# Row sums of a self-attention layer: partial sums kept by DMAs are added on VectorE instead of being summed by TensorE, and the DMAs' blocks lie two to three places earlier

## The chip, the cores and the metric

The kernel runs on one core of one Trainium2 chip. The metric is device time in microseconds, the median of several runs of the same program. Three runs of the kernel before took 3301.09, 3304.72 and 3309.56 us.

## The reference

Two layers work on an image batch `x` of shape (2, 256, 64, 64). Each is `x = x + layer(groupnorm(x))`. Layer 1 (block attention and a 3x3 convolution) is not touched here. Layer 0 is full self-attention over the 4096 pixels of each image, with 8 heads of 32 channels:

```python
qkv = jnp.einsum('bchw,oc->bohw', x, qkv_w) + qkv_b[None, :, None, None]
qkv = qkv.reshape(b, 3, num_heads, head_dim, n)
q, k, v = (qkv[:, 0], qkv[:, 1], qkv[:, 2])
attn_logits = jnp.einsum('bhci,bhcj->bhij', q, k) * scale
attn_weights = jax.nn.softmax(attn_logits, axis=-1)
out = jnp.einsum('bhij,bhcj->bhci', attn_weights, v)
```

The softmax needs, for each query, the sum of its 4096 exponentials. How these sums are taken is the subject.

## The kernel before

**Units, blocks, groups.** For one image, layer 0 is cut into 16 groups `g`: head `g // 2` and one half of the queries (2048 of them, in 4 units `u` of T = 512). A group has NJ = 32 blocks `j`, each of 128 keys. Block `j` of a group is four *units*: score tiles of 128 keys x 512 queries. For each unit TensorE makes the scores (L426) into PSUM, ScalarE takes the exponential of two or three units at once (L432), and TensorE multiplies the result with the values (L442, tile `av`). That last product has only 32 output rows, so the four units of a block are written to four quarters of one PSUM bank (`quarters`, L438). The two images follow one another, so layer 0 has 32 groups in all; layer 1 of each image comes after its layer 0.

**The ring.** Exponentials lie in a ring of 28 places (RING, L378), which is seven blocks or four batches of scores. A place is written again four batches later, so by then everyone who reads it must be done: TensorE, VectorE, and DMAs.

**The row sums.** Summing over the 4096 keys has two steps. First, the 32 blocks of a group are added element by element, so that 128 x 512 partial sums stay for each unit. Then a product with a matrix of ones sums over the 128 partitions. The element-by-element part is split in two:

- VectorE adds most blocks into two tiles `added[g]` (`e` in the profile, L471 to L479), two units (128 x 1024) in one instruction.
- The seven blocks in `SUMMED` (L380) are added by DMAs that accumulate, issued from GpSimd (`add_in_memory`, L481): the first of a group is a plain copy (L487), the others add (L489). They go to four buffers `acc`, which lie in tiles of several names, so the profile calls them `es`, `v` and `acc`.

`sum_rows` (L502) then multiplies both with `ones`: one product of four quarters for `acc`, one for `added`, into one spare bank of the score tile `sa`. In the last group of an image `finish_last` (L538) does the same with two blocks more.

**What follows.** `finish(g)` (L509) takes the row sums on: ScalarE copies them out (L515), a DMA brings them to DRAM and back in a dense form (L516, L518), VectorE takes minimum, maximum and reciprocal (L521 to L523), DMAs bring the reciprocals back, spread over partitions (L524, L526), and VectorE multiplies the group's output with them (L530). Each of these steps has its place in the next group: the sums after block 1 has been worked on, the reciprocal after block 8, the multiplication after block 13.

**The order of work.** `tc.manual_schedule` (L635) keeps the order in which instructions are written for TensorE, ScalarE and VectorE. The loop at L643 writes one batch of 7 units of scores and exponentials, then as many steps of older blocks as a fixed share allows (`steps`, L609). [...] SyncE's queue has the plain DMAs: in even groups it fetches the next head's keys and values at block 4 (L622, `fetch_head`), and at the end of each group the queries of the group after the next (L631).

Around the change, the sums of group `g` are asked for after block 1 of group `g + 1` (L615), and are written once two more steps have been written, which is at block 3 or 4. `waiting` is a check of the program's writer: `acc` may not be overwritten before the sums have read it.

Of the kernel before, what the change touches and what calls it, by code (L numbers as in the profile page):

```python
# [40 lines left out]
def direct_layers(ctx: ExitStack, tc: tile.TileContext, a: dict, out: bass.AP, bad: bass.AP):  # L41
# [3 lines left out]
    nc = tc.nc  # L45
# [13 lines left out]
    def w4(shape, name, dtype=F32):  # L59
        return work.tile(shape, dtype, tag="w4", name=name)  # L60
# [159 lines left out]
    ones = const.tile([P, HD0], F32, name="ones")  # L220
# [81 lines left out]
    def fetch_head(b, h, held):  # L302
        r = slice(HD0 * h, HD0 * h + HD0)
        kt = kpool.tile([P, N], F32R, tag="kv", name=f"k_{b}_{h}")
        for g in range(4):
            nc.sync.dma_start(
                out=kt[HD0 * g : HD0 * g + HD0, :].bitcast(F32), in_=halves["wk0"][b][g // 2, r, :]
            )
        held["k", h] = kt
        nc.sync.dma_start(out=held["v"][:, h % 2, :, :], in_=vals[b][:, :, r])  # L310

    def fetch_queries(b, g, held):
        h, p = divmod(g, 2)
        r = slice(HD0 * h, HD0 * h + HD0)
        for w in range(2):
            qt = w4([P, 2, T], f"q_{b}_{g}_{w}", F32R)
            n0 = (4 * p + 2 * w) * T
            for q in range(4):
                nc.sync.dma_start(
                    out=qt[HD0 * q : HD0 * q + HD0].rearrange("p s n -> p (s n)").bitcast(F32),  # L320
                    in_=halves["wq0"][b][q % 2, r, n0 : n0 + 2 * T],
                )
            held["q", g, w] = qt
# [53 lines left out]

    RING, RING_A = 28, 17  # L378

    SUMMED = (5, 9, 13, 17, 21, 25, 28)  # L380


    SUMMED_LAST = (NJ - 2, NJ - 1)

    def attention0(b, xts, held):
# [6 lines left out]
        pair = cpool.tile([P, 2, T], F32, tag="col", name=f"acc_{b}")  # L392

        acc = [es[:, RING_A, :], held["acc"][:, 0, :], pair[:, 0, :], pair[:, 1, :]]
        vals2 = held["v"]
        n_units = NH0 * 2 * NJ * 4
        sums, added, copied = {}, {}, {}
        waiting = []
        last = NH0 * 2 - 1
# [4 lines left out]
        def at_places(first, n):  # L404

            while n > 0:
                at = first % RING
                m = min(n, (RING_A if at < RING_A else RING) - at)
                yield m, es[:, at : at + m, :] if at < RING_A else held["es"][:, at - RING_A : at - RING_A + m, :]
                first, n = first + m, n - m  # L410
# [27 lines left out]
        def quarters(dst, lhs, rhs, start, stop, part=None):  # L438

            n = slice(0, T) if part is None else slice(part * T // 2, (part + 1) * T // 2)  # L440
            for u in range(4):
                nc.tensor.matmul(dst[HD0 * u : HD0 * u + HD0, n], lhs, rhs(u)[:, n], start=start, stop=stop)  # L442

        def unit(g, j, u):
            ((_, e),) = at_places(places[(g * NJ + j) * 4 + u], 1)
            return e[:, 0, :]
# [10 lines left out]
        def add_rows(g, j):  # L457
# [4 lines left out]
            for w in range(2):  # L462
                dst = added[g][w]
                if j in SUMMED:
                    if w == 0:
# [15 lines left out]
        def add_in_memory(g, j):  # L481
            assert not waiting or j != SUMMED[0]
            runs = [(acc[u].unsqueeze(1), unit(g, j, u).unsqueeze(1)) for u in (0, 1)]
            runs += [(pair[:, s, :], src) for s, src in two_units(g, j, 1)]
            for dst, src in runs:
                if j == SUMMED[0]:
                    nc.gpsimd.dma_start(out=dst, in_=src)  # L487
                else:
                    nc.gpsimd.dma_start(out=dst, in_=src, accum_op=ALU.add)  # L489

        def work_of(g, j):


            add_rows(g, j)
            for part in (None,) if j in (0, NJ - 1) else range(2):
                if part == 1:
                    yield
                quarters(
                    sums[g], held["v"][:, (g // 2) % 2, j, :], lambda u: unit(g, j, u), j == 0, j == NJ - 1, part
                )  # L500

        def sum_rows(g, rows):  # L502
            waiting.clear()
            quarters(rows, ones, lambda u: acc[u], True, False)
            for j in SUMMED_LAST if g == last else ():
                quarters(rows, ones, lambda u: unit(g, j, u), False, False)
            quarters(rows, ones, lambda u: added[g][u // 2][:, u % 2, :], False, True)

        def finish(g):  # L509

            h, p = divmod(g, 2)
            rows = yield
            sum_rows(g, rows)
            avs = copied[g]
            nc.scalar.copy(avs[:, 1, :], rows)  # L515
            nc.sync.dma_start(out=dsum[b][g], in_=avs[0:P:HD0, 1, :])  # L516
            dense = small.tile([P, 4 * T // P], F32, tag="dense", name=f"dense_{b}_{g}")
            nc.sync.dma_start(out=dense, in_=dsum[b][g].rearrange("u (q n) -> (u q) n", n=4 * T // P))  # L518
            yield
            at = b * NH0 * 2 + g  # L520
            nc.vector.tensor_reduce(span[:, 0, at : at + 1], dense, AX.X, ALU.min)  # L521
            nc.vector.tensor_reduce(span[:, 1, at : at + 1], dense, AX.X, ALU.max)
            nc.vector.reciprocal(dense, dense)  # L523
            nc.sync.dma_start(out=drec[b][g].rearrange("u (q n) -> (u q) n", n=4 * T // P), in_=dense)  # L524
            for u in range(4):
                nc.sync.dma_start(  # L526
                    out=avs[HD0 * u : HD0 * u + HD0, 1, :], in_=drec[b][g, u].partition_broadcast(HD0)
                )
            yield
            nc.vector.tensor_mul(avs[:, 0, :], avs[:, 0, :], avs[:, 1, :])  # L530
            for u in range(4):
                nc.sync.dma_start(
                    out=ctx0[b][HD0 * h : HD0 * h + HD0, (4 * p + u) * T : (4 * p + u + 1) * T],
                    in_=avs[HD0 * u : HD0 * u + HD0, 0, :],
                )
            yield
# [72 lines left out]
        def steps():  # L609

            for done in range(NH0 * 2 * NJ):
                g, j = divmod(done, NJ)
                for _ in work_of(g, j):
                    yield done
                if g and j == 1:  # L615
                    wanted.append(late[0].send)
                    waiting.append(g)
                if g and j in (8, 13):
                    next(late[0])
                for what in also.get((g, j), ()):  # L620
                    what()
                if j == 4 and g % 2 == 0 and g // 2 + 1 < NH0:  # L622
                    fetch_head(b, g // 2 + 1, held)
                if j == NJ - 1:
                    avs = w4([P, 2, T], f"avs_{b}_{g}")
                    nc.scalar.copy(avs[:, 0, :], sums[g])
                    copied[g] = avs
                    late[:] = [finish(g)]
                    next(late[0])
                    if g + 2 < NH0 * 2:  # L630
                        fetch_queries(b, g + 2, held)  # L631
                yield done + 1

        E = mybir.EngineType
        with tc.manual_schedule(engines={E.PE, E.Activation, E.DVE}):  # L635

            per_group = 2 * NJ - 2
            work, begun, taken = steps(), 0, 0  # L640
            scores(False)
            final = False
# [977 lines left out]
def kernel(tc: tile.TileContext, a: dict, out: bass.AP):  # L1620
    nc = tc.nc
    with tc.tile_pool(name="verdict", bufs=1) as verdict:
        bad = verdict.tile([1, 1], I32, name="bad")
        direct_layers(tc, a, out, bad)
        redo = nc.values_load(bad[0:1, 0:1])
        with tc.If(redo > 0):
            general_layers(tc, a, out)
# [79 lines left out]
```

## Time and profile before

The profiled execution has a span of 3295.2 us. Layer 0 of the two images runs from about 110 to 1175 us and from about 1757 to 2817 us. Both stretches look alike.

| Stretch (us) | Length | PE busy | DVE busy | ACT busy | POOL busy |
|---|---|---|---|---|---|
| 190 to 1140, layer 0, first image | 950 | 941.18 | 817.89 | 876.32 | 256.54 |
| 1160 to 1760, layer 1 and projections | 600 | 537.55 | 347.21 | 200.46 | 135.24 |
| 1760 to 2809, layer 0, second image | 1049 | 1042.47 | 906.49 | 969.18 | 285.57 |
| 2809 to 3295, layer 1, second image | 486 | 433.44 | 210.00 | 143.28 | 119.09 |

A row of such a table is read across: the engine whose busy time comes closest to the length is the first suspect for the bound of that stretch, and the others show how much room they have. In the lists of groups, a line names the code line, engine, operation, tiles and shapes, then how many there were, their busy time in us and the mean of one in ns, and, after the second bar, the idle time just before them with what ended it.

### The profile page before, as it was taken

To read this page: it belongs to the slowest core of one execution; us is meant where nothing else is said; L and a number is where in the kernel's file an instruction comes from. 1 tells how busy PE (TensorE), PEld (TensorE's weight loads), DVE (VectorE), ACT (ScalarE), POOL (GpSimd) and SP (SyncE) were. 2 spreads that over 40 slices of the span, in tenths; PEclk is the share of its full clock that TensorE was granted. 3 is DMA by queue.
4 is the path that set the end of the run, shared out by engine and by line. 5 is a ranking of instruction groups with operands and counts; after the bars stand their busy time and mean duration, and the time that the engine had idled before them with its cause. 6 is when DMAs were issued, how large, how long until landed. Compare 5 with 4: busy or idle time off the path is not lost. (4 is left out here: it accounts for less than half of the span.)

```text
span 3295.2 us, 62532 instructions
## 1 busy us (share of the span) xinstructions
PE 3139.2 (95%) x25113; PEld 1844.7 (56%) x25113; DVE 2416.1 (73%) x3138; ACT 2310.7 (70%) x2354; POOL 843.4 (26%) x929
## 2 busy tenths in 40 slices
PE   7999999999999979999979999999999999799998
PEld 4455555555555535666654555555555555356665
DVE  4688888888989888554446887978889898424454
ACT  2798999999989943422227999999999999424222
POOL 2122222223222210444201222222222222005331
PEclk9999999999999979999989999999999999799999
DMA  7967878689776631300159678787797776200000
GB/s 258 251 136 152 168 144 181 145 158 183 143 163 139 141 76 47 134 26 26 45 187 255 137 153 171 142 175 153 158 185 144 156 145 139 79 2 10 14 13 27
DMA packets 243917, 425.23 MB, mean 129 GB/s; under 512 B 99009, under 2 KB 109593, under 8 KB 241185
## 3 DMA queue, kind: packets, MB, share of 16 engines
q0 software_dynamic: 98336, 241.20, 37.8%
q1 hardware_dynamic: 145280, 179.93, 20.5%
q8 instruction: 199, 3.26, 0.4%
q14 instruction: 102, 0.83, 0.1%
HBM read 118.26 MB, written 67.86 MB: 56 GB/s over the span
## 5 line engine op out<-in xcount | busy, mean ns | idle before, releaser
L479 DVE TENSOR_TENSOR e<-e,es 128x1024 f32<-128x1024 f32 (+1 forms) x950 | 1034.4, 1149 | 57.2 <-ACT es L432 57.0
L442 PE MATMUL av<-es,v 128*32 128x256 f32 (+1 forms) x9644 | 745.6, 390 | 0.0
L432 ACT ACTIVATE es<-sa 128x1536 f32<-128x1536 f32 (+1 forms) x444 | 635.6, 1431 | 92.3 <-PE sa L426 47.7
L479 DVE TENSOR_TENSOR e<-e,v 128x1024 f32<-128x1024 f32 (+1 forms) x630 | 668.9, 1118 | 22.7 <-ACT v L432 22.3
L426 PE MATMUL sa<-q,k 128*128 128x512 f32 x1736 | 561.1, 430 | 13.7 <-issue 4.5
L442 PE MATMUL av<-v 128*32 128x256 f32 (+1 forms) x6228 | 506.9, 389 | 0.0
L442 PEld LDWEIGHTS av<-es,v 128*32 128x32 f32 x9644 | 316.2, 109 | 299.4 <-issue 160.2
L426 PEld LDWEIGHTS sa<-q,k 128*128 128x128 f32 x1736 | 279.9, 188 | 297.0 <-issue 139.9
L426 PE MATMUL sc<-q,k 128*128 128x512 f32 x1180 | 373.1, 397 | 7.2 <-ACT es L432 4.3
L426 PE MATMUL sb<-q,k 128*128 128x512 f32 x1180 | 371.3, 396 | 2.1 <-ACT es L432 1.6
L442 PEld LDWEIGHTS av<-v 128*32 128x32 f32 x6228 | 216.3, 109 | 178.5 <-issue 81.5
L432 ACT ACTIVATE es<-sc 128x1024 f32<-128x1024 f32 x296 | 306.8, 1037 | 3.8 <-DVE e L479 3.8
L432 ACT ACTIVATE v<-sc 128x1024 f32<-128x1024 f32 x294 | 304.9, 1037 | 0.4 <-DMA es<-v 0.2
L432 ACT ACTIVATE es<-sb 128x1024 f32<-128x1024 f32 x296 | 302.1, 1021 | 2.9 <-DMA acc<-es 2.9
L432 ACT ACTIVATE v<-sb 128x1024 f32<-128x1024 f32 x294 | 300.1, 1021 | 2.6 <-DMA acc<-v 1.4
L426 PEld LDWEIGHTS sc<-q,k 128*128 128x128 f32 x1180 | 209.0, 187 | 83.6 <-ACT es L432 17.3
L426 PEld LDWEIGHTS sb<-q,k 128*128 128x128 f32 x1180 | 220.2, 188 | 59.0 <-ACT es L432 4.1
L489 POOL DMA_DIRECT2D es<-es x118 | 101.4, 859 | 523.4 <-ACT es L432 468.5
L801 POOL TENSOR_TENSOR v<-col 128x512 f32<-128x512 f32 x128 | 167.0, 1330 | 264.7 <-DMA out_dram<-res_sr 116.9
L432 ACT ACTIVATE v<-sa 128x1536 f32<-128x1536 f32 (+1 forms) x146 | 209.2, 1433 | 33.4 <-PE sa L426 15.2
L811 PE MATMUL mm<-v,wf 128*128 128x256 f32 x1024 | 226.6, 379 | 2.2 <-POOL v L801 1.2
L816 ACT COPY z<-mm 128x512 f32<-128x512 f32 x32 | 18.7, 585 | 283.8 <-PE mm L811 268.3
(241 smaller groups left out, 3519.0 us busy)
## 6 DMA issues: line engine op xcount, KB each, us to landing
acc<-es POOLq DMA_DIRECT2D x122, 512.0 KB, 6.1
acc<-v POOLq DMA_DIRECT2D x76, 512.0 KB, 6.3
es<-es POOLq DMA_DIRECT2D x136, 256.0 KB, 3.8
v<-es POOLq DMA_DIRECT2D x132, 256.0 KB, 4.6
k<-wk_halves SPq DMA_DIRECT2D x64, 512.0 KB
q<-wq_halves SPq DMA_DIRECT2D x256, 128.0 KB
v<-v POOLq DMA_DIRECT2D x92, 256.0 KB, 4.8
es<-v POOLq DMA_DIRECT2D x88, 256.0 KB, 3.8
```

The lines of the kernel that those rows point to most:

```text
L426: nc.tensor.matmul(sc[:, i, :], held["k", g // 2][:, j * P : (j + 1) * P], held["q", g, u // 2][:, u % 2, :], start=True, stop=True,)
L432: nc.scalar.activation(dst, sc[:, i : i + m, :], AF.Exp, scale=SC0)
L442: nc.tensor.matmul(dst[HD0 * u : HD0 * u + HD0, n], lhs, rhs(u)[:, n], start=start, stop=stop)
L479: nc.vector.tensor_add(dst[:, s, :], dst[:, s, :], src)
L489: nc.gpsimd.dma_start(out=dst, in_=src, accum_op=ALU.add)
L801: (nc.gpsimd.tensor_add if plus else nc.gpsimd.tensor_sub)(dst, rows(one), rows(two))
L811: nc.tensor.matmul(mm[:, m, r, :], wf[:, k, 4 * r + q, m * P : (m + 1) * P], v[r // 2][:, r % 2, k, :], start=k == 0, stop=k == KC - 1,)
L816: nc.scalar.copy(z[:, 1], mm[:, :, 1, :])
```

## The change

The list `SUMMED` moves forward: 5, 9, 13, 17, 21, 25, 28 becomes 3, 7, 11, 15, 18, 22, 26. There are still seven blocks in it. In every group but the last of an image, `sum_rows` no longer multiplies `acc` with ones; instead VectorE, at block 0 of the next group, adds `acc` into `added` with three instructions (two of 128 x 512 and one of 128 x 1024), and the one remaining product reads `added` alone. The last group of an image keeps its two products (and those of its last two blocks). The `waiting` check follows the new reader of `acc`.

```diff
-    SUMMED = (5, 9, 13, 17, 21, 25, 28)
+    SUMMED = (3, 7, 11, 15, 18, 22, 26)
...
         def sum_rows(g, rows):
-            waiting.clear()
-            quarters(rows, ones, lambda u: acc[u], True, False)
-            for j in SUMMED_LAST if g == last else ():
-                quarters(rows, ones, lambda u: unit(g, j, u), False, False)
-            quarters(rows, ones, lambda u: added[g][u // 2][:, u % 2, :], False, True)
+            if g == last:
+                quarters(rows, ones, lambda u: acc[u], True, False)
+                for j in SUMMED_LAST:
+                    quarters(rows, ones, lambda u: unit(g, j, u), False, False)
+            quarters(rows, ones, lambda u: added[g][u // 2][:, u % 2, :], g < last, True)
...
                 for _ in work_of(g, j):
                     yield done
+                if g and j == 0:
+
+                    for w in range(2):
+                        dst = added[g - 1][w]
+                        for s in range(2) if w == 0 else (slice(0, 2),):
+                            nc.vector.tensor_add(dst[:, s, :], dst[:, s, :], acc[s] if w == 0 else pair)
+                    waiting.clear()
                 if g and j == 1:
                     wanted.append(late[0].send)
-                    waiting.append(g)
...
                 if j == NJ - 1:
+                    waiting.append(g)
                     avs = w4([P, 2, T], f"avs_{b}_{g}")
```

## The prediction

> **What bounds the kernel now.** I read three views in this order: busy time by stretch, for the engine that has no room; the groups of instructions by line, for the price of one; the timeline of a group's seam and of a wait, for what hides what.
>
> ```profile
> 190.00:1140.00 950.00, 941.18 (x9172) 528.40 (x9174) 817.89 (x835) 876.32 (x835) 256.54 (x313) 1.00 0.78 155
> 1760.00:2809.00 1049.00, 1042.47 (x10149) 587.49 (x10149) 906.49 (x912) 969.18 (x916) 285.57 (x349) 1.00 0.79 158
> ```
>
> Columns: stretch, length, then busy us (and instructions) of PE, PE's weight loads, DVE, ACT, POOL, then clock, DMA share, GB/s. In the first layer-0 stretch PE is busy 941.18/950 = 99%, ACT 92%, DVE 86%. Starts of L515 in the timeline (row sums copied out, once per group) lie (2755.86 - 1836.52)/14 = 65.7 us apart, that is 2.05 us per block. Per group ACT works 0.922 x 65.7 = 60.6 us, DVE 0.861 x 65.7 = 56.6 us. So **PE bounds layer 0**; ACT has 5 us of room per group and DVE 9.
>
> ```profile
> 586.55 0.59 PE L442 MATMUL sa<-v,ones 128*32 128x512 f32 x1
> 587.40 1.04 PE L442 MATMUL sa<-e,ones 128*32 128x512 f32 x8
> 588.26 0.61 PE L442 MATMUL av<-v 128*32 128x256 f32 x8
> ...
> 588.51 0.58 ACT L515 COPY avs<-sa 128x512 f32<-128x512 f32 x1 [0.82 <-PE sa L442]
> ...
> 590.04 6.89 DVE L479 TENSOR_TENSOR e<-e,es 128x1024 f32<-128x1024 f32 x6
> ```
>
> This is the seam of one group (start, duration, what). The product of `acc` starts at 586.54, that of `e` at 587.40, the next `av` at 588.26: each ones-product holds PE for 0.86 us, back to back, with no wait in it. The last line gives the DVE's pace: six adds in 6.89 us, so (6.89 - 1.215)/5 = 1.135 us each when they follow one another, 2.27 us per block of two, **more than the 2.05 us in which a block is made**. DVE falls behind in a run of its own blocks and catches up at those that DMAs add.
>
> ```profile
> DVE avs L530 <- DMA avs<-drec: 145.7, 24, 10.6
> ...
> POOL es L487 <- PE sa L442: 519.5, 30, 19.9
> ...
> 810.73 0.69 DVE L530 TENSOR_TENSOR avs<-avs 128x512 f32<-128x512 f32 x1 [9.98 <-DMA avs<-drec]
> ...
>   DVE e L479: 10.9, 16
> ```
>
> First two: waits by pair (total us, times, longest). At block 13 the DVE stands still for the reciprocals, 6.1 us on average in 24 of 30 groups, with adds queued behind. The third is one such wait, 9.98 us in an even group, where the fetch of the next head (issued at block 4) is ahead of `drec`. The last is from the list of what ended ACT's idle time at L432: 16 waits for a DVE add, 10.9 us in all, since a place of the ring was still being read. They lie just after such waits (L530 ends at 811.4; blocks 14 to 20 of that group are done within 0.1 to 1.3 us of their place's next writing). So DVE is already at its limit in some even groups, but only there.
>
> [...] I checked the steps: 0.2166 us each, and over the 258 batches of scores of each image the time above the median batch comes to only 13.1 and 6.5 us. The trace agrees that PE really is issuing. [...] the four quarters start within 0.02 us, and a product's 8 instructions cost two steps of 0.43, not eight. [...]
>
> **The change, part by part** (against the profiled span, 3295.2 us).
>
> 1. *Product of `acc` removed.* Groups of L442: 240 `sa<-e,ones` over 8 per product = 30 groups; the same 240 for `acc` (120 + 60 + 60) go. 30 x 0.86 = **-25.8 us**, on the path. The rest of the seam follows: ACT's copy L515 waited 0.82 us for PE, 24.4 us in 30, so it can start 0.8 us sooner; at most 0.05 us a group is lost to ACT.
>
> 2. *Three adds on DVE per group.* 0.68 + 0.68 + 1.14 = 2.50 us (rows of L479), 30 groups, 75 us. DVE then needs 59.1 of 64.8 us per group. Hidden? They stand between block 31 and the next group's first add. PE needs `added` at its ones-product: from the DVE's end of block 31 to the first ones-product I read 3.4 us (first image, group 2) to 12.3 us, so 0.9 us stays at the worst: **0**. Behind them, blocks 0 and 1 come 2.5 us later; the tightest place there has 2.97 us until its next writing (group 11). From block 3 on, which DVE no longer adds, it is level again: before the reciprocal at block 8 it now does six blocks and the three adds, in place of seven blocks (+0.2 us).
>
> 3. *New wait: DVE's adds on the landing of the last accumulation,* with the whole DVE queue behind. POOL's last issue of block 28 ended 5.3 to 12.0 us before DVE finished block 31; block 26 is two blocks, 4.1 us, sooner. So 9.4 us or more, against a landing of 6.0 (longest 12.4): **0**; at worst 3 us in a few groups where DVE has no backlog.
>
> 4. *DMA blocks moved.* Nothing is removed: seven blocks, three or four POOL issues each. The first of a group (L487) waited for PE's product (519.5 us in 30, harmless); now it waits for DVE's adds. Block 3's exponentials and the adds are both done 9.7 to 14 us before the ring needs the places; the seam, shorter by 0.86, lies inside that. Issue takes 1.7 us and landing 6.0, so some 1.1 us stays in the tightest (groups after even ones); a landing of 12.4 would stall up to 5. I take **+1 us** in all, bounds 0 and 12. Past SP's queue: the accumulations near the head fetch were those of blocks 5, 9 and 13, now 3, 7 and 11; about two still fall into it.
>
> 5. *DVE blocks around the wait at block 13.* Before it come 9, 10, 12, 13 in place of 10, 11, 12: one block, 2.27 us, more work inside a wait of 6.1, which pays most of the 75 us (24 x 2.27 = 54). After it block 14 is as late as before, but every following block has one add fewer ahead of it. The ring waits of 10.9 us shrink: **-2 us**, bounds 0 and -11.
>
> Sum: -25.8 + 0 + 0 + 1 - 2 = -26.8, so 3268.4 for the profiled span. That execution lies 9.5 us under the median of 3304.7 (its spread is 8.5); from the median: **3278 us**.
>
> **Rivals.**
>
> - *More:* ring waits vanish too, -37: **3267**. For: later blocks gain 2.27 us. Against: block 14 gains nothing.
> - *Half:* block 3's accumulations land late, or the worst seams have DVE behind; about 1 us in each of 12 groups: **3290**. For: the 0.9 and 1.1 us left over. Against: these are single groups; most keep 3 us.
> - *No gain:* ACT or DVE is right behind PE, so what PE saves is waited away: **3304**. For: ACT at 92%. Against: 5 us of room, and ACT's waits at L432 are mostly for PE.
> - *Slower:* the reciprocals come later in even groups[...]. There are 12 such groups, and there DVE is at the ring's limit, so each us goes to PE. Break-even at 25.8/12 = 2.2 us; a delay of 4 us costs 48 - 26 = +22: **3327**. For: waits of 7 to 10 us there show a crowded queue. Against: blocks 5 and 9 met the same fetch, as many bytes.
> - *That the change does nothing* would need the `acc` product to lie in idle PE time; the seam shows none.
>
> **How the numbers follow.** Forecast (3271 to 3285) 62%, more 14%, half 13%, no gain 5%, slower 6%. Range 3266 to 3291: it takes in most of "more" and "half" and leaves out about 2 in 10. A measurement of this kernel tells about 0.3% (10 us) from no change. Faster by more, below 3294.8: the first two cases and most of "half", 88%; within 0.3% 7%; slower 5%.
>
> **What would show it.** In the profile after: 240 `ones` matmuls of tile `sa` (`e` alone); L515 starts about 64.8 us apart; PE still at 99% in layer 0, DVE near 91%; the total of `DVE avs L530 <- DMA avs<-drec` falls from 145.7 to some 95 us or less; ACT's waits for DVE adds below 10.9. It would be wrong if PE's loads at `sa<-e,ones` wait for a DVE add, if ACT waits for `DMA acc` for more than the 6.2 us of now, or if L530 comes later than 27 us after L515 in even groups.

## The result, and the profile after

The kernel after takes 3288.9 us (median of four runs, 3284.8 to 3292.9) against 3304.9 us before: 16.0 us less, ratio 0.9951 with a 95% interval of 0.9933 to 0.9969. Forecast were 26.8 us less. Repeated on another chip it came to the same, 3288.7 and 0.9951 (0.9936 to 0.9965). The direction was right and the time lies inside the range, near the rival that kept half of the gain. About 10 us are missing, and it turned out that they hide a larger sum.

The page of the kernel after, then its busy time by stretch (columns as above):

```profile
span 3286.0 us, 62212 instructions
PE 3119.0 (95%) x24873; PEld 1840.3 (56%) x24873; DVE 2484.2 (76%) x3244; ACT 2309.7 (70%) x2354; POOL 829.5 (25%) x913
```

```profile
190.00:1140.00 950.00, 936.29 (x9106) 529.01 (x9096) 855.39 (x891) 879.73 (x839) 251.29 (x307) 1.00 0.78 155
1760.00:2809.00 1049.00, 1036.62 (x10128) 587.05 (x10127) 947.63 (x974) 972.20 (x919) 278.93 (x341) 1.00 0.79 158
```

PE has exactly the 240 matmuls less (25113 to 24873), as forecast; DVE is up 68 us, where 75 were forecast. But PE is busy for 936.29 of the same 950 us, where it was 941.18: it now has *more* gaps than before. The seam of a group is as planned (timeline: start, duration, engine, line):

```profile
586.92 0.69 DVE L620 TENSOR_TENSOR e<-e,es 128x512 f32<-128x512 f32 x1
587.52 0.69 DVE L620 TENSOR_TENSOR e<-e,v 128x512 f32<-128x512 f32 x1
588.12 1.22 DVE L620 TENSOR_TENSOR e<-e,acc 128x1024 f32<-128x1024 f32 x1
...
591.66 1.04 PE L442 MATMUL sa<-e,ones 128*32 128x512 f32 x8
...
592.77 0.59 ACT L515 COPY avs<-sa 128x512 f32<-128x512 f32 x1
```

The three adds end at 589.3, 2.3 us before the one product that reads them; PE waits for none of them. So the gaps are elsewhere. The list of waits names them:

```profile
DVE avs L530 <- DMA avs<-drec: 92.6, 17, 9.5
...
POOL acc L489 <- DMA acc<-es: 63.7, 32, 4.4
...
POOL acc L489 <- DMA acc<-v: 50.7, 25, 4.4
```

DVE's wait for the reciprocals fell from 145.7 to 92.6 us, as forecast. GpSimd's wait for one accumulation to land before it issues the next into the same buffer rose from 77.5 (40.5 + 37.0) to 114.4 us. What ended ACT's idle time at L432, before: DVE adds 10.9 us, DMAs of `acc` 6.2. After:

```profile
  DVE e L479: 14.0, 10
  issue: 11.1, 9
  DMA acc<-es: 9.5, 6
  DMA v<-es: 6.1, 2
```

ACT finds its place in the ring still being read, now by DMAs too. Two of the three signs that the prediction gave for being wrong are there: more waits for DMAs, and L530 30.9 us after L515 in group 4 of the first image.

Cutting each image at the first scores, the first L515 and the last L515 shows where the time went (us, from the profiles; the kernels e2 to e12 are those of the next section):

| Kernel | Image 1: group 0 | groups 1 to 15 | Image 2: group 0 | groups 1 to 15 |
|---|---|---|---|---|
| before | 79.2 | 925.5 | 79.1 | 919.4 |
| after | 82.1 | 920.8 | 82.6 | 908.3 |
| e2, adds, old blocks | 78.9 | 909.6 | 76.9 | 906.3 |
| e4, after, old blocks in group 0 | 79.4 | 917.7 | 77.6 | 912.6 |
| e7, after, late values | 82.8 | 908.8 | 83.3 | 906.4 |
| e10, both | 79.2 | 915.2 | 77.7 | 906.9 |
| e12, both, even spacing | 78.9 | 909.4 | 77.4 | 908.0 |

A row is one execution, and two of them are fast ones: the profiles of before and e7 lie 7.4 and 6.4 us under the median of their kernel. In the long columns, differences of a few us tell nothing. Group 0 is steadier: 82.1 to 83.9 us in the four profiles that have block 3 in it, 76.9 to 80.3 in the other ten.

The distances from one L515 to the next say more. Twelve of them begin in a group that fetches a head (groups 2, 4, ... 12 of each image), sixteen in one that does not. Their means in us, worked out from the same traces:

| | before | after | e2 | e4 | e5 | e6 | e7 | e8 | e9 | e10 | e12 |
|---|---|---|---|---|---|---|---|---|---|---|---|
| 12 with a fetch | 66.5 | 66.4 | 65.1 | 66.6 | 66.0 | 66.4 | 65.3 | 65.8 | 64.9 | 65.8 | 65.3 |
| 16 without | 65.4 | 64.5 | 64.6 | 64.5 | 64.5 | 64.5 | 64.5 | 65.4 | 64.5 | 64.5 | 64.6 |

Without a fetch, every kernel that lost the product is 0.8 to 0.9 us a group faster, whatever its list. What goes beyond that, gain or loss, lies in the groups with a fetch and in group 0.

Group 0 of each image, where 0.9 us should have been saved, became 3 us longer. In its first microseconds (timeline of PE, then of ACT and POOL):

```profile
129.79 0.62 PE L426 MATMUL sb<-q,k 128*128 128x512 f32 x2
133.69 1.22 PE L426 MATMUL sc<-q,k 128*128 128x512 f32 x2 [3.28 <-ACT es L432]
134.84 3.64 PE L442 MATMUL av<-es,v 128*32 128x256 f32 x32
```

```profile
127.79 0.89 POOL L489 DMA_DIRECT2D es<-es  x1 [8.97 <-DMA es<-es]
...
132.62 1.02 ACT L432 ACTIVATE es<-sc 128x1024 f32<-128x1024 f32 x1 [3.47 <-DMA v<-es]
```

GpSimd sits 9 us until the copies of block 3 have landed, ACT waits 3.5 us for a place that such a copy still reads, and PE has no scores to make. In the kernel before, GpSimd sat as long, and it did no harm:

```profile
119.89 0.58 POOL L487 DMA_DIRECT2D es<-v  x1 [12.79 <-ACT v L432]
...
132.81 0.89 POOL L489 DMA_DIRECT2D es<-es  x1 [10.42 <-DMA es<-v]
```

There the last copy landed at 134.2 us. In the kernel after the copies are issued 3 us earlier and the last lands at 134.7, no sooner, while its place is due two blocks (4.1 us) earlier. Then PE pays twice: its next two matmuls take 1.22 us in place of 0.62, at a lower granted clock:

```profile
132.00:139.20 7.20, 5.50 (x36) 2.58 (x37) 2.45 (x2) 4.31 (x4) 2.56 (x3) 0.53 1.28 219
```

The granted clock is 0.53 in this stretch; in e4, where group 0 has the old blocks, it is 1.00, and PE makes 64 matmuls in the same 7.2 us in place of 36. In the kernel after the clock fell at 132.3 us, 1.9 us into a gap of 3.28, and stayed at half until 139.1. The last section comes back to this.

### The profile page after: what moved, and what is told of

It reads as the page before. It is cut to its first block, busy times and chain, and to the rows that moved or that the text cites. A ratio compares the mean times of both kernels' runs of the same rounds, so it can differ in the third digit from the quotient of the medians.

```text
span 3286.0 us, 62212 instructions
## 1 busy us (share of the span) xinstructions
PE 3119.0 (95%) x24873; PEld 1840.3 (56%) x24873; DVE 2484.2 (76%) x3244; ACT 2309.7 (70%) x2354; POOL 829.5 (25%) x913
## 5 line engine op out<-in xcount | busy, mean ns | idle before, releaser
L479 DVE TENSOR_TENSOR e<-e,es 128x1024 f32<-128x1024 f32 (+1 forms) x956 | 1034.2, 1142 | 33.2 <-ACT es L432 32.8
L432 ACT ACTIVATE es<-sa 128x1536 f32<-128x1536 f32 (+1 forms) x444 | 635.9, 1432 | 96.4 <-PE sa L426 51.8
L479 DVE TENSOR_TENSOR e<-e,v 128x1024 f32<-128x1024 f32 (+1 forms) x640 | 673.1, 1108 | 27.1 <-ACT v L432 27.0
L432 ACT ACTIVATE es<-sc 128x1024 f32<-128x1024 f32 x296 | 306.5, 1035 | 14.6 <-DVE e L479 8.5
L432 ACT ACTIVATE v<-sc 128x1024 f32<-128x1024 f32 x294 | 304.4, 1036 | 1.4 <-DMA acc<-v 1.2
L432 ACT ACTIVATE es<-sb 128x1024 f32<-128x1024 f32 x296 | 302.3, 1021 | 3.3 <-DMA acc<-es 3.3
L432 ACT ACTIVATE v<-sb 128x1024 f32<-128x1024 f32 x294 | 300.1, 1021 | 2.2 <-DVE e L479 2.2
L432 ACT ACTIVATE v<-sa 128x1536 f32<-128x1536 f32 (+1 forms) x146 | 209.4, 1434 | 33.8 <-PE sa L426 15.8
```

What stands on the lines that cost most here:

```text
L432: nc.scalar.activation(dst, sc[:, i : i + m, :], AF.Exp, scale=SC0)
L479: nc.vector.tensor_add(dst[:, s, :], dst[:, s, :], src)
```

## The experiments

Each row of times is a median; ratios are to the kernel before on the same chip, with 95% intervals. There were three theories: the moved blocks' DMAs meet other transfers (DMA theory), the adds load VectorE too much (VectorE theory), or the product was worth less.

**e1: no product, no adds, old blocks.** Edit to the kernel before:

```diff
-            quarters(rows, ones, lambda u: acc[u], True, False)
+            if g == last:
+                quarters(rows, ones, lambda u: acc[u], True, False)
...
-            quarters(rows, ones, lambda u: added[g][u // 2][:, u % 2, :], False, True)
+            quarters(rows, ones, lambda u: added[g][u // 2][:, u % 2, :], g < last, True)
```

> The kernel before with the product of acc left out in all but the last group of an image and nothing in its place (the DMAs still add into acc, nobody reads it; the row sums lack the seven DMA blocks). Three theories for the 10 us that are missing from the forecast. DMA theory: the product is worth its full 26 us, and the moved blocks give 8 to 10 us back because the DMAs of blocks 3, 7 and 11 meet other transfers; VectorE theory: the product is worth 26 us, and the three adds give 10 us back; small-product theory: removing the product is worth only some 16 us. Against 3304.9 us before: DMA and VectorE theories 3279 (3274 to 3284), small-product theory 3289.

Measured: 3269.2 us, 0.9897 (0.9881 to 0.9912). That is 36 us, and 10 more than any theory said.

**e2: adds in place of the product, old blocks** (the kernel after, with the list undone):

```diff
-    SUMMED = (3, 7, 11, 15, 18, 22, 26)
+    SUMMED = (5, 9, 13, 17, 21, 25, 28)
```

> The change without its list: SUMMED stays 5, 9, 13, 17, 21, 25, 28, the adds on VectorE replace the product. DMA theory: nothing is given back by the moved blocks, 3280 (3275 to 3285), group 0 of each image as long as before (79.2 us from the first scores to the first L515, less 0.9) where after has 82. VectorE theory: 3289 or more, since the adds cost as they do after, and VectorE has one block less of work inside its wait at block 13.

Measured: 3267.6 us, 0.9894 (0.9876 to 0.9912). As fast as e1: **the three adds on VectorE cost nothing** that can be measured, and the change without its list gains 37 us. The list takes 21 us of that back.

**e3: new blocks, no adds.** Edit to the kernel after:

```diff
-                        for s in range(2) if w == 0 else (slice(0, 2),):
-                            nc.vector.tensor_add(dst[:, s, :], dst[:, s, :], acc[s] if w == 0 else pair)
```

> The kernel after with the three adds on VectorE left out (the row sums of all but the last group of an image lack the seven DMA blocks). DMA theory: the loss stays, 3287 (3284 to 3291), group 0 about 82 us. VectorE theory: 3279, and no wait of ScalarE for VectorE at the ring beyond those of before.

Measured: 3290.1 us, 0.9952 (0.9938 to 0.9966), group 0 at 82.3 and 83.5 us. Without the adds the loss stays whole. The VectorE theory falls.

**e4: new blocks, but old ones in group 0.**

```diff
+    SUMMED_FIRST = (5, 9, 13, 17, 21, 25, 28)
...
-                if j in SUMMED:
+                if j in summed(g):
...
+        def summed(g):
+            return SUMMED_FIRST if g == 0 else SUMMED
```

> The kernel after, but group 0 of each image keeps the old blocks 5, 9, 13, 17, 21, 25, 28. DMA theory: group 0 gets back the 3 to 4 us that it lost in each image, 3282 (3278 to 3286), group 0 about 78.5 us from first scores to first L515; the waits in even groups stay. VectorE theory: as after, 3289, since the adds are all there.

Measured: 3282.0 us, 0.9927 (0.9913 to 0.9942). Group 0 is back at 79.4 and 77.6 us. Some 7 us of the loss sit in the two groups 0.

**e5: only the first three blocks new** (`3, 7, 11, 17, 21, 25, 28`, group 0 as in e4), and **e6: only the last four** (`5, 9, 13, 16, 19, 22, 26`, group 0 as in e4).

> As e4 (group 0 keeps the old blocks), but in the other groups only the first three blocks are the new ones: 3, 7, 11, 17, 21, 25, 28. Head-fetch theory (blocks 7 and 11 are added by DMAs while the next head is fetched in even groups): nearly all of what e4 loses against e2 stays, 3280 (3276 to 3285). Spacing theory (three blocks from 15 to 18 are too few for one accumulation after another, or the later blocks load VectorE badly): as e2, 3268 (3264 to 3272).

> The counterpart of e5: group 0 keeps the old blocks; elsewhere 5, 9, 13 are the old ones and 16, 19, 22, 26 stand for the new ones 15, 18, 22, 26 (one place later, so that they do not follow 13 too closely). Head-fetch theory: as e2, 3268 (3264 to 3272). Spacing theory: as e4, 3282.

Measured: e5 3278.4 us, 0.9921 (0.9904 to 0.9938), as the head-fetch theory said. But e6 3282.4 us, 0.9934 (0.9921 to 0.9946), where it expected 3268. So the places of blocks 3, 7 and 11 can't be all. e6 has three gaps of three blocks (13, 16, 19, 22), and GpSimd's waits for `acc` rose to 154 us (92.0 + 61.8), twice those before. My list for e6 was thus no clean counterpart; it made spacing a suspect of its own. But e6 loses in the groups with a fetch alone (66.4 us against 65.1 in e2); in the others it is as fast as e2 (64.5 and 64.6).

**e7 and e8: the call of `fetch_head` moved from block 4 to block 16**, in the kernel after and in the kernel before:

```diff
-                if j == 4 and g % 2 == 0 and g // 2 + 1 < NH0:
+                if j == 16 and g % 2 == 0 and g // 2 + 1 < NH0:
```

> The kernel after, with the fetch of the next head in even groups at block 16 instead of block 4 (behind the reciprocals on SyncE's queue). Head-fetch theory: blocks 3, 7 and 11 no longer meet it, the reciprocals come at 16 to 21 us after L515 in even groups too, and the wait of VectorE at L530 falls below 30 us: 3268 (3260 to 3274). VectorE or spacing theory: 3289, since neither adds nor blocks change.

> The kernel before with the fetch of the next head at block 16 instead of block 4. If the extra 10 us that e1 and e2 gained over the 26 us of the product come from block 5's copies getting away from the head fetch, the kernel before gets about these 10 us by this edit: 3295 (3290 to 3299). If they are part of the product's own price, the time stays at 3305.

The edit moves less than its text says. `manual_schedule` (L635) names TensorE, ScalarE and VectorE, not SyncE, and a fetch is five transfers: four of keys (L306) and one of values (L310). Group 4 of the first image, before, then e8:

```profile
391.36 0.68 SPq L306 DMA_DIRECT2D k<-wk_halves  x1
...
395.29 0.59 SPq L310 DMA_DIRECT2D v<-vals  x1
398.07 5.21 SPq L524 DMA_DIRECT2D drec<-dense  x1
```

```profile
389.57 0.66 SPq L306 DMA_DIRECT2D k<-wk_halves  x1
...
396.20 0.34 SPq L524 DMA_DIRECT2D drec<-dense  x1
396.64 0.59 SPq L310 DMA_DIRECT2D v<-vals  x1
```

In every group with a fetch, with either edit, two transfers of keys are issued 13 to 19 us before L515 and two 1 to 5 us after it. Only the values move: from 3.2 to 5.3 us after L515, ahead of L524, to 7.6 to 13.4 us, behind it. So **e7 to e12 test the place of the values' transfer** (512 KB, in 4096 packets of 128 bytes), not that of the whole fetch; "late fetch" and "late values" mean this here.

Measured: e7 3281.4 us, 0.9933 (0.992 to 0.9946). Short of the 3268, because group 0 keeps its loss (82.8 and 83.3 us), which my expectation forgot. In its profile, the fastest of its five runs, groups 1 to 15 take the 909 and 906 us of e2, and the wait at L530 falls to 47.7 us, not below 30. e8: 3291.1 us, 0.9964 (0.9951 to 0.9977). So **the kernel before loses 11 us to the place of the values' transfer**, and its runs, spread over 8.5 us, lie within 2.4 us once that is moved. It does not gain through DVE's wait at L530 (145.7 us before, 144.8 in e8). What changes are the landings: accumulations issued 3 to 14 us after L515 in a group with a fetch land after 9.0 us in the median before and 6.2 in e8; in groups without a fetch it is 4.9 and 4.8. ACT's waits for DVE adds fall from 10.9 to 0.4 us.

**e9: e2 with the same edit.**

> e2 (three adds for the product, old blocks) with the head fetch at block 16, so it stands to e8 as the product stands to the adds, with no head fetch near. Head-fetch theory: the product's clean price, 30 x 0.86 = 26 us under e8's, that is 37 us under the kernel before on the same chip (3266, 3262 to 3270), and about the same as e2, which had already got away from the fetch. If the product is worth more than its own time even without the fetch: 3258 or less.

Measured: 3266.3 us, 0.9888 (0.9871 to 0.9905). Against e8 that is 24.8 us: the product's clean price, 26 forecast. Against e2 the edit gains no more than noise. So e2 had already got away from what costs the kernel before 11 us.

**e10: the kernel after with both cures** (old blocks in group 0, late values), and **e12: the same with even spacing:**

```diff
-    SUMMED = (3, 7, 11, 15, 18, 22, 26)
+    SUMMED = (3, 7, 11, 15, 19, 23, 27)
```

> The kernel after with both edits: group 0 of each image keeps the old blocks (e4), and the head fetch is at block 16 (e7). If the loss of the new blocks has just these two parts, nothing of it is left: 3266 (3261 to 3271), group 0 at 78 us in each image and groups 1 to 15 at 909 and 906 us from first to last L515. If the new blocks cost anything else: 3272 or more.

> As e10 (group 0 with the old blocks, head fetch at block 16), but the other groups add blocks 3, 7, 11, 15, 19, 23, 27 by DMA: four blocks apart everywhere, where e10 has 15, 18 (three apart, in the middle of the late fetch). If the 8 us that e10 still lacks to e9 are GpSimd waiting for one accumulation to land before the next of the same buffer: 3267 (3263 to 3271), and GpSimd's waits for acc (132 us in e10, 51 in e9) fall below 90. If they come from blocks 3, 7 and 11 themselves: as e10, 3274.

Measured: e10 3274.0 us, 0.991 (0.9897 to 0.9924), still 7.6 behind e9. e12 3267.1 us, 0.9887 (0.9871 to 0.9904): nothing is left. The waits of GpSimd for landings, e10 first and e12 second:

```profile
POOL acc L493 <- DMA acc<-es: 76.0, 36, 3.8
...
POOL acc L493 <- DMA acc<-v: 56.4, 26, 4.4
```

```profile
POOL acc L493 <- DMA acc<-es: 43.6, 27, 3.6
...
POOL acc L493 <- DMA acc<-v: 33.0, 19, 3.4
```

132 us became 77, by moving three blocks one place each. **Three blocks were too few between accumulations where a fetch ran beside them**: a block takes 2.05 us, so 15 to 18 leaves 6.1 us, and an accumulation needed 6.2 us to land in the median (the longest landing, of a copy in group 0, took 16.5, both in the kernel after). Where no fetch ran, gaps of three blocks cost nothing (e6 and e10, 64.5 us a group; e12 64.6). That it is the gap, and not the later places of these three blocks, rests on e6 and on GpSimd's waits; it was not tried apart.

**e11: the kernel after once more.**

> The kernel after once more, unchanged, so that it stands on the same chip as the two above: 3289 (3284 to 3293).

Measured: 3288.7 us, 0.9951 (0.9936 to 0.9965).

The list's 21 us thus lie in two places: some 7 in the two groups 0 (e4), the rest in the twelve groups with a fetch. On one way through the experiments that rest falls into two steps, 8 us for the values' transfer (e4 to e10) and 7 for the spacing (e10 to e12), each good to some 4 us. But the order matters: with the fetch as it was, taking away the gap from 15 to 18 gave 3.6 us, not clear of noise (e4 to e5), and e7, which has e10's code in all groups but 0, was in its profile as fast as e12 there. So the two act together, and how the rest divides between them stays open; that nothing remains is clear (e12 as e9 and e2). e2, e9 and e12 are the fastest versions, some 21 us below the kernel after.

## Why the prediction was right and wrong

The time came out inside the range partly by luck: the sum had left out a gain of some 11 us and put a loss of 21 at 1, and these offset each other by half.

- *Step 1, the product: right.* 25.8 us forecast, 24.8 between e8 and e9; in the groups without a fetch 0.8 to 0.9 us each, 0.86 forecast. L515 starts (2746.13 - 1837.82)/14 = 64.9 us apart in the second image, where 64.8 were forecast, but 920.8/14 = 65.8 in the first.
- *Step 2, the adds: right.* e1 and e2 are equal within the noise, and so are e3 and after.
- *Step 3, the new wait of DVE on landings: right* in what it cost; the trace of e2 has 3.5 us of it, in two waits, and e2 loses nothing against e1.
- *Step 4, the moved blocks: wrong*, and this is the step that failed. It put +1 us with bounds 0 and 12; the runs show 21 (e2 against after). Its room of "9.7 to 14 us" was read from groups 1 to 15 alone. Group 0 has no group before it and lies in the image's opening transfers, where the copies took 11.3 to 12.4 us to land in the kernel before and 10.3 to 16.5 in the kernel after. Its sentence that "about two still fall into" the head fetch counted the blocks but not when they are issued, nor that the fetch is not one piece at block 4: half of the keys are issued before, the values last. And it never priced 15 to 18 being three apart, where the old list had its one such gap at its end, 25 to 28. The wait of 9.98 us that the prediction showed lies behind the fetch in SyncE's own queue, and says nothing of GpSimd's transfers beside a fetch; their landings do: in the kernel before, accumulations took 9.0 us in the median beside a fetch and 4.9 elsewhere.
- *Also step 4: the released copies were called harmless, and that hid a gain.* The first copy of a group waited for PE's product (519.5 us in 30), and the prediction took that as idle time that costs nothing. But it ended just ahead of the two later transfers of keys and that of the values. Group 4 of the first image, in the kernel before (POOL, then SP):

```profile
389.54 0.57 POOL L487 DMA_DIRECT2D es<-es  x1 [19.83 <-PE sa L442]
...
391.36 0.68 SPq L306 DMA_DIRECT2D k<-wk_halves  x1
```

and in e2:

```profile
380.33 0.57 POOL L487 DMA_DIRECT2D es<-es  x1 [14.28 <-ACT es L432]
...
385.94 0.44 SPq L306 DMA_DIRECT2D k<-wk_halves  x1
```

  The copies start 1.8 us before the later part of the fetch in the one, 5.6 in the other. Over the twelve groups with a fetch they start 0.7 us ahead of L515 in every group before, and 1.5 to 5.4 us (3.2 on average) in e2. There L530 comes 24.6 us after L515 on average in e2, 25.7 before, 26.7 after. That e1 and e2 gained some 11 us over the product's own price, and that these 11 vanish once the values' transfer is moved (e8 to e9: 25), shows that this transfer is in it. That it is the copies' earlier start was not tried by itself; it fits the lines above.
- *Step 5, less work after the wait: not seen.* ACT's waits for DVE adds went from 10.9 to 14.0 us, not down, and L530 comes 1.0 us later in the groups with a fetch. In e2, with the old blocks, they fell to 3.4 us (2.3 at L479, 1.1 at L471), so the moved blocks did not help here. The sign "later than 27 us" was a weak one: in the kernel before, L530 already came 27.9 us after L515 in one such group.
- *The rivals.* "Half" was the number (3290), and one of its two grounds was right, late landings of block 3, but in group 0 and not in the worst seams. "Slower" named the right groups and the fetch, but there L530 is 1 us later on average, not 4.

## What to carry to other kernels

Price a moved DMA by what is in flight where it lands, in every group and above all the first (in the kernel before, accumulations landed after 9.0 us in the median beside a fetch and 4.9 elsewhere, the copies in group 0 after 11.3 to 12.4). A wait that ends just ahead of a big transfer may decide whether the two meet (the copies of group 4 started 1.8 us before the later part of the fetch in the kernel before and 5.6 in e2, not tried by itself), so it isn't harmless because its engine is idle. After an edit that moves a transfer, look in the trace where each of its parts went: here the call moved by twelve blocks, and of five transfers only the values' went behind L524. Compare like parts of the program (here groups with and without a fetch) before comparing whole spans. Accumulations into one buffer waited for each other's landings, 114.4 us of GpSimd's time in the kernel after: leave more room between them than a median landing. Beside a fetch 6.1 us of room against a median of 6.2 went with a loss, and four blocks, 8.2 us, with none. When a change joins a rearrangement to a saving, run each alone: here the saving was worth 37 us, and the rearrangement took 21 of them.

## What the runs showed of the hardware

In four places of the kernel after, a gap on PE cost more than itself. In group 4 of the first image PE waits 4.5 us, and then its granted clock is 0.50 for 3.41 us more, from 425.84 us on:

```profile
425.71 1.13 PE L426 MATMUL sc<-q,k 128*128 128x512 f32 x2 [4.50 <-ACT es L432]
426.77 2.70 PE L442 MATMUL av<-es,v 128*32 128x256 f32 x24
```

```profile
425.80:429.20 3.40, 3.40 (x26) 1.29 (x26) 3.40 (x4) 3.28 (x3) 1.57 (x2) 0.51 0.12 26
```

The 24 quarter products take 2.70 us here and 1.50 us at full clock (at 140.56 us). In its two layers 0 the kernel after has four such stretches, from 132.29, 289.31, 425.84 and 1791.17 us on, of 6.83, 3.41, 3.41 and 3.41 us at half clock; the kernel before has none.

The length of the gap alone does not decide it. At the same place in group 2, the kernel after, then the kernel before:

```profile
288.37 0.73 PE L426 MATMUL sc<-q,k 128*128 128x512 f32 x2 [1.86 <-ACT es L432]
```

```profile
286.07 0.73 PE L426 MATMUL sc<-q,k 128*128 128x512 f32 x2 [1.92 <-ACT es L432]
```

In the kernel after the clock halves at 289.31 us; before, after a longer gap, it does not. In the 3.41 us ahead of each of the four falls PE was busy 45, 45, 4 and 31% of the time, for example:

```profile
285.90:289.31 3.41, 1.55 (x13) 0.67 (x15) 3.41 (x4) 1.91 (x2) 0.52 (x1) 1.00 0.97 183
```

That share alone does not decide it either. Around the longer gap of the kernel before, PE was busy for 44% of an equal stretch, and the clock stayed at 1.00 in it and in the 3.41 us behind it:

```profile
283.60:287.01 3.41, 1.49 (x13) 0.60 (x15) 3.41 (x4) 1.91 (x2) 0.70 (x1) 1.00 0.77 171
287.01:290.42 3.41, 3.41 (x41) 1.99 (x33) 3.41 (x5) 2.70 (x4) 1.89 (x3) 1.00 0.82 142
```

What does decide it stays open here.
